# Unread matmuls in TensorE's waits, and another order of the last scatters, in a four-layer kernel with experts

## The chip, the cores and the metric

The kernel runs on one core of one Trainium2 chip. The metric is the device time of one execution in microseconds (us); the time before is the median of three runs. A profiled execution, of which the trace is kept, has a time of its own.

## What is computed

The input is x of 4 x 1024 tokens with 256 features. Four sub-layers follow each other, each as x = x + layernorm(f(layernorm(x))): a gated attention in groups of 64 with a cumulative linear part, a low-rank feed-forward, an attention of 16 heads with relu weights, and a layer of experts. The change touches the seam between the last two and the end of the last one:

```python
# attention: scores = relu(q k / 4), divided by their sum, times v
S = sigmoid(xt @ Wg).T                    # 8 experts x 4096 tokens
G, I = top_k(S, 1024)                     # each expert takes its 1024 best tokens
hid = gelu(ex @ W1[e] + b1[e])            # ex = xt[I], 1024 x 256 -> 1024
out = (hid @ W2[e] + b2[e]) * G[..., None]
new_x = zeros.at[I].add(out)              # summed over the experts
x = x + layernorm(new_x)
```

## The kernel before

The tokens are held in eight tiles xs[0..7] of 512 tokens (128 partitions x 4 x 256). TensorE, VectorE and ScalarE run in the order in which the program is written (manual schedule, L1040 and L1315); GpSimd's order is the program's too from the seventh expert on (L1753).

**The relu attention (to L1307).** A loop over batch, query half, head group and key tile does scores (L1226), relu, and one step later the weighting with v (L1242). Other work is kept in two lists of closures, `beside` (steps with matmuls) and `rest` (vector steps); `go_on` (L1255) takes one of `beside` and one or two of `rest` after each step of the loop. After the loop, `finish` (L1304) does the last weighting and puts `divide` in front of `rest`: transposes on VectorE (L1274, L1113) that make oT. Then `while beside or rest: go_on()` (L1305) works off the lists: the output projection of tile 7 (pt, L1128), the transposes and gate matmuls of tile 6 (tpg L1186, pg L1200), tile 7's two layernorms on VectorE, ScalarE and GpSimd, and tile 7's own tpg and pg.

**The gate (L1319 to L1438).** Sigmoid of the logits (L1346 to L1349); a transpose of the scores (scoreT, `by_token` L1354), which are stored beside the token rows in tok_d; 15 rounds of a search for the threshold of each expert, three compares with counts on VectorE and one small matmul with the 0/1 matrix same_b (pn, L1381) each; a mask, two matmuls for counts (pall L1409, pearly L1411), two scans, and a transpose of the places (placeT, L1354 again, called at L1432). From the places come hi and lo, and from these the list of an expert's tokens: 32 small matmuls (parts, L1478) fed by VectorE's compares (at, L1468), one matmul with fold (L1490), the index on VectorE, and eight indirect DMAs from GpSimd's queue that fetch the rows (got, L1502).

**The experts (L1676).** 16 units u, two for each expert, of 512 tokens: transposes of the fetched rows (`turn`, L1672), W1 (ph, L1690), gelu (L1697), W2 (py, L1713), and the scatter with addition into acc_d (L1732). The first unit is done in two halves. The list of the next expert is made inside the first unit of each expert.

**The last expert.** Its sums aren't scattered into acc_d. While it runs, all other rows of acc_d are read back tile by tile, normalised, added to x and stored (`all_stats`, `all_scaled`, `all_out`). For its own 1024 tokens, in eight groups k of 128, the accumulated rows are fetched (`fetch_acc`), the bias times the gate is added (`known`, L1589), then this expert's py (L1726), then statistics with a power on GpSimd (`chosen_stats`, L1543 to L1547: rsd), subtraction of the mean (L1598), the sum with x (`chosen_sum`, L1602), and a scatter from GpSimd's queue over rows of the output (`chosen_out`, L1606), which waits for all stores of `all_out`. The table `beside_last` (L1631) says after which step these are issued: (half, "f", i) after the i-th block of W1, (half, "i", i) after the sum of k = 4 x half + i. Engines take what they are issued in that order, so a power stands in GpSimd's queue behind the scatters that were listed before it.

## Time and profile before

| what | value |
|---|---|
| three runs | 1636.32, 1636.36, 1637.09 us (median 1636.36) |
| the profiled execution's own time | 1637.27 us |
| its span, first to last instruction | 1635.4 us |
| busy: PE, DVE, ACT, POOL | 1544.9, 920.3, 634.4, 403.1 us |
| mean granted TensorE clock | 0.974 |
| PE busy from 1090 to 1140 us | 8.9 us of 50 |
| end of PE's last matmul, of the last scatter's issue | 1622.58, 1629.75 us |

PE is TensorE's matmuls, DVE is VectorE, ACT ScalarE, POOL GpSimd, SP the engine that issues most DMAs. The clock is given as a share of full speed. A matmul of f32 operands is two records in the trace. "Idle before, releaser" says how long an engine had nothing to do before an instruction and what ended that.

### The profile page before, as it was taken

The numbers are of one execution on the slowest core, as the hardware profiler recorded it, in microseconds if no ns is written. First come the engines' busy times: TensorE is split into PE (matmuls) and PEld (weight loads), VectorE is DVE, ScalarE is ACT, GpSimd is POOL, SyncE is SP. The second block draws the span as 40 slices with busy tenths as digits, with TensorE's granted clock in tenths as the row PEclk, the third lists the DMA queues.
The fourth block names the chain that finished last, engine by engine and source line by source line (L and its number), as shares of the span: only waits on it lengthen the run. The fifth ranks groups of instructions, "written<-read, shape, count | busy, mean of one in ns | idle before, by whom it ended". The sixth has DMA issues, their size and how long they took to land.

```text
span 1635.4 us, 22372 instructions
## 1 busy us (share of the span) xinstructions
PE 1544.9 (94%) x8663; PEld 769.3 (47%) x8663; DVE 920.3 (56%) x2085; ACT 634.4 (39%) x1101; POOL 403.1 (25%) x439
## 2 busy tenths in 40 slices
PE   7999999999999999999999999941999999999996
PEld 4666666665222232222323222220757667566674
DVE  5555566663657787878787888868211212122145
ACT  3344444445444545454545454511121121211232
POOL 4123232322201020111111101110423324323554
PEclk9999999999999999999999999965899999999998
DMA  8300000000000000001010100040233233234364
GB/s 202 122 1 1 1 1 1 1 1 1 1 1 1 27 14 15 25 7 34 6 35 1 40 9 19 14 167 4 54 77 69 66 74 72 66 77 94 60 156 124
DMA packets 70069, 71.13 MB, mean 43 GB/s; under 512 B 23598, under 2 KB 62923, under 8 KB 69835
## 3 DMA queue, kind: packets, MB, share of 16 engines
q1 hardware_dynamic: 56080, 47.01, 9.3%
q0 software_dynamic: 13008, 21.77, 7.2%
q8 instruction: 68, 1.11, 0.3%
q10 hardware_dynamic: 874, 0.93, 0.2%
q14 instruction: 39, 0.31, 0.1%
HBM read 41.74 MB, written 27.95 MB: 43 GB/s over the span
## 4 chain that ended last, share of the span: by engine, by line
PE 90%; issue 4%; DVE 3%; POOL 1%; ACT 1%; DMA 1%; SPq 0%; POOLq 0%; ACTq 0%; DVEq 0%
PE sc L1226 16%; PE po L1242 16%; PE ph L1690 13%; PE py L1713 13%; PE py L792 4%; PE pg L684 3%; PE pv L700 3%; PE pt L1128 2%; PE ph L848 2%; PE po L764 2%; PE pv L373 2%; PE pq L349 2%; PE pq L869 2%; PE po L768 2%; PE pk L349 2%
## 5 line engine op out<-in xcount | busy, mean ns | idle before, releaser
L1236 DVE TENSOR_SCALAR w<-sc 128x1024 f32<-128x1024 f32 x256 | 312.6, 1222 | 97.5 <-PE sc L1226 65.1
L1235 ACT ACTIVATE w<-sc 128x512 f32<-128x512 f32 x512 | 277.9, 594 | 229.7 <-PE sc L1226 102.5
L1226 PE MATMUL sc<-qT,kT 32*128 32x512 f32 x2048 | 293.6, 639 | 1.5 <-ACT w L1235 0.8
L1242 PE MATMUL po<-w,vaug 128*17 128x512 f32 x2048 | 274.7, 598 | 1.3 <-DVE turned L1274 0.3
L1713 PE MATMUL py<-w,hid 128*128 128x256 f32 x1024 | 230.1, 380 | 0.0
L1690 PE MATMUL ph<-xT,w 128*128 128x512 f32 (+1 forms) x544 | 225.0, 572 | 0.5 <-DVE xT L1674 0.4
L1697 ACT ACTIVATE hid<-ph,mb 128x512 f32<-128x512 f32 (+1 forms) x136 | 90.0, 662 | 346.3 <-PE ph L1690 345.0
L1713 PEld LDWEIGHTS py<-w,hid 128*128 128x128 f32 x1024 | 191.1, 190 | 32.0 <-issue 7.3
L1226 PEld LDWEIGHTS sc<-qT,kT 32*128 32x128 f32 x2048 | 80.8, 183 | 184.9 <-issue 170.7
L1690 PEld LDWEIGHTS ph<-xT,w 128*128 128x128 f32 x544 | 104.8, 193 | 111.7 <-issue 107.6
L1242 PEld LDWEIGHTS po<-w,vaug 128*17 128x17 f32 x2048 | 35.3, 95 | 200.3 <-issue 171.0
L1732 POOL DMA_INDIRECT acc_d<-y,idx x56 | 88.5, 1580 | 156.6 <-issue 129.4
L1502 POOL DMA_INDIRECT got<-tok_d,idx x64 | 65.8, 1027 | 154.1 <-DVE idx L1492 137.0
L1730 DVE TENSOR_TENSOR y<-py,mb 128x256 f32<-128x256 f32 x56 | 23.4, 418 | 142.7 <-PE py L1713 140.6
L1674 DVE COPY xT<-tp 128x512 f32<-128x512 f32 (+1 forms) x34 | 22.3, 660 | 93.4 <-PE tp L1672 93.4
L1060 POOL TENSOR_TENSOR rsg<-veg,mhalf 128x1 f32<-128x1 f32 x32 | 17.7, 553 | 219.6 <-DVE veg L1059 219.6
L792 PE MATMUL py<-wo,oT 128*128 128x256 f32 x256 | 61.9, 385 | 0.0
L684 PE MATMUL pg<-nT,wh 128*128 128x512 f32 x128 | 60.5, 604 | 1.5 <-ACT nT L623 1.5
L700 PE MATMUL pv<-wh,nT 128*128 128x512 f32 x128 | 59.7, 592 | 0.0
L1492 DVE CAST idx<-parts 128x8 int32<-128x8 f32 x8 | 1.3, 167 | 101.8 <-PE parts L1490 101.8
L792 PEld LDWEIGHTS py<-wo,oT 128*128 128x128 f32 x256 | 47.3, 190 | 17.2 <-issue 9.4
L565 POOL TENSOR_TENSOR x<-x,y 128x1024 f32<-128x1024 f32 x14 | 32.9, 2352 | 73.3 <-ACT y L554 73.3
(275 smaller groups left out, 1888.8 us busy)
## 6 DMA issues: line engine op xcount, KB each, us to landing
w<-in_L_ffn_W_dram SPq DMA_DIRECT2D x16, 1024.0 KB, 5.7
x<-in_L_attn_x_dram SPq DMA_DIRECT2D x8, 512.0 KB, 4.8
acc_d<-logits SPq DMA_DIRECT2D x8, 512.0 KB, 4.2
x_d<-x SPq DMA_DIRECT2D x8, 512.0 KB, 2.9
tok_d<-hg SPq DMA_DIRECT2D x32, 128.0 KB, 1.7
back_w<-acc_d SPq DMA_DIRECT2D x6, 512.0 KB, 8.0
out_dram<-x SPq DMA_DIRECT2D x20, 128.0 KB, 1.7
out_dram<-back_w POOLq DMA_DIRECT2D x4, 512.0 KB
```

The lines of the kernel that those rows point to most:

```text
L684: nc.tensor.matmul(pg, lhsT=wh[:, c, HID + e * P : HID + (e + 1) * P], rhs=d["nT"][:, c, :], start=(c == 0), stop=(c == DC - 1),)
L700: nc.tensor.matmul(pv, lhsT=d["nT"][:, c, i * P : (i + 1) * P], rhs=wh[:, c, 0:HID], start=(c == 0), stop=(c == DC - 1),)
L792: nc.tensor.matmul(py, lhsT=d["oT"][:, e, :], rhs=wo[:, e, :], start=(e == 0), stop=(e == EC - 1))
L1226: nc.tensor.matmul(sc, lhsT=row["kT"][t][rows, r, kt * P : (kt + 1) * P], rhs=row["qT"][rows, t, qh * TB : (qh + 1) * TB], start=True, sto ...
L1235: nc.scalar.activation(w[:, j, :], sc, AF.Relu)
L1236: nc.vector.tensor_scalar(w[:, 2:4, :], pair, 0.0, None, ALU.max)
L1242: nc.tensor.matmul(po[32 * j : 32 * j + HD + 1, :], lhsT=row["v"][:, kt, HQ * t + 2 * j + r, :], rhs=w[:, j, :], start=(kt == 0), stop=(kt ...
L1502: return nc.gpsimd.indirect_dma_start(out=dst, out_offset=None, in_=rows[:, :], in_offset=self.at_chunk(c), bounds_check=NT - 1, oob_is_er ...
L1690: nc.tensor.matmul(ph, lhsT=w1[:, c, f * P : (f + 1) * P], rhs=xT[u][:, c, h * n : (h + 1) * n], start=(c == 0), stop=(c == DC - 1),)
L1697: nc.scalar.activation(hid[:, f, h * n : (h + 1) * n], ph, AF.Gelu, bias=mb1[:, e * FC + f : e * FC + f + 1])
L1713: nc.tensor.matmul(py, lhsT=hid[:, f, i * P : (i + 1) * P], rhs=w2[:, f, :], start=(f == 0), stop=(f == FC - 1),)
L1732: scatter = nc.gpsimd.indirect_dma_start(out=acc_d[:, :], out_offset=lists[e].at_chunk(k), in_=y, in_offset=None, bounds_check=NT - 1, oob ...
```

## The change

One helper is new: it issues n matmuls of 128 x 128 by 128 x 512, bf16, same_b with itself (as the moving operand repeated four times), into a PSUM bank that nobody reads. It is called at seven places, with 8, 63, 9, 13, 12, 15 and 4 matmuls (124 in all). The loop that works off `beside` and `rest` after the attention is split, so that two of the calls stand ahead of it and after the first emptying of `beside`. The table of the last expert lists `known` 4 to 7, `chosen_sum` and `chosen_out` at other steps and in another order within a step.

```diff
+    def keep_busy(bank, n):
+        for _ in range(n):
+            nc.tensor.matmul(
+                bank, lhsT=same_b, rhs=same_b.unsqueeze(1).to_broadcast([P, 4, P]), start=True, stop=True
+            )
...
         finish(*before)
+        idle = ps.tile([P, 2, TB], F32, tag="d", name="idle", bufs=2)[:, 0, :]
+        keep_busy(idle, 8)
+        while rest and not beside:
+            go_on()
+        while beside:
+            go_on()
+
+        keep_busy(idle, 63)
         while beside or rest:
             go_on()
...
             nc.vector.reciprocal(sc, sc)
+            idle = ps.tile([P, TB], F32, tag="idle", name="idle", bufs=1)
+            keep_busy(idle, 9)
...
             nc.tensor.matmul(pearly, lhsT=earlier_b, rhs=n, start=True, stop=True)
+            keep_busy(idle, 13)
...
                 place, by_token(upto, "placeT").rearrange("p k (s e) -> p (k s) e", e=NE), -1.0, None, ALU.add
             )
+            keep_busy(idle, 12)
...
-            (1, "f", 5): [(all_scaled, 7, front), (all_out, 6)],
+            (1, "f", 5): [(all_scaled, 7, front), (all_out, 6), (known, 4)],
             (1, "f", 6): [(all_scaled, 7, back), (chosen_less_mean, 0, 1, 2, 3)],
-            (1, "f", 7): [(all_out, 7), (known, 4, 5, 6, 7)],
-            (1, "i", 0): [(chosen_sum, 0, 1, 2, 3), (chosen_stats, 4), (chosen_less_mean, 4), (chosen_out, 0, 1, 2, 3)],
-            (1, "i", 1): [(chosen_sum, 4), (chosen_stats, 5), (chosen_less_mean, 5), (chosen_out, 4)],
-            (1, "i", 2): [
-                (chosen_sum, 5), (chosen_out, 5), (chosen_stats, 6), (chosen_less_mean, 6), (chosen_sum, 6), (chosen_out, 6)
+            (1, "f", 7): [(all_out, 7), (chosen_sum, 0, 1, 2, 3)],
+            (1, "i", 0): [(chosen_stats, 4), (chosen_less_mean, 4), (chosen_out, 0, 1), (known, 5), (chosen_sum, 4)],
+            (1, "i", 1): [
+                (chosen_stats, 5), (chosen_less_mean, 5), (chosen_out, 2, 3, 4), (known, 6, 7), (chosen_sum, 5),
             ],
+            (1, "i", 2): [(chosen_stats, 6), (chosen_less_mean, 6), (chosen_out, 5), (chosen_sum, 6), (chosen_out, 6)],
             (1, "i", 3): [(chosen_stats, 7), (chosen_less_mean, 7), (chosen_sum, 7), (chosen_out, 7)],
...
                 nc.tensor.transpose(tp[:, i, :], lists[e].got[q * NJ + i][:, c * P : (c + 1) * P], ident)
+                if u == 0 and c == 0 and i == 0:
+
+                    keep_busy(first, 4)
...
         lists[0].gather()
+        first = ps.tile([P, TB], F32, tag="mm", name="idle", bufs=3)
+        keep_busy(first, 15)
```

## The prediction

> **What bounds the kernel now.** I read the page's busy slices first, then the windows, the waits and the chain around the dip, then the time line of the end.

> ```profile
> PE   7999999999999999999999999941999999999996
> ...
> PEclk9999999999999999999999999965899999999998
> ```
> TensorE fills the span but for one dip (slices 26 to 28, about 1068 to 1155 us) and the last slice; in the dip its granted clock falls to half. Only these two places can be bought. Windows of 3.413 us, laid so that the clock changes at their edges (start:end, length, PE busy, ..., then clock, DMA share, GB/s):

> ```profile
> PE tpg L1186 <- DVE hg L1171: 14.8, 1, 14.8
> PE tp L1672 <- DMA got<-tok_d,idx: 4.6, 2, 3.7
> PE scoreT L1354 <- DVE sc L1349: 3.9, 1, 3.9
> PE placeT L1354 <- DVE upto L1428: 3.5, 1, 3.5
> PE parts L1478 <- DVE at L1468: 3.2, 1, 3.2
> PE pt L1128 <- DVE oT L1113: 2.3, 1, 2.3
> ```
> These six waits are where the fillers go; each is how long one may last. And the chain (start, us):

> ```profile
> 1149.16 9.44 PE ph L1690 x32
> ...
> 1159.43 7.14 PE ph L1690 x32
> ```
> The same 32 matmuls take 9.44 us from a cold start and 7.14 us warm. (Further pieces of the chain used below: pt's 14 records 4.99 us from 1071.49; the next expert's 32 parts matmuls, warm, 1.92 us.) At the end (time line; start, us, [idle before]):

> ```profile
> 1621.49 0.58 POOL L1547 TENSOR_TENSOR rsd<-ved,mhalf 128x1 f32<-128x1 f32 x1
> 1622.10 0.48 DVE L1602 SCALAR_TENSOR_TENSOR xg<-accg,rsd,xg 128x256 f32<-128x256 f32 x1 [2.46 <-POOL rsd L1547]
> ...
> 1625.83 0.48 DVE L1726 SCALAR_TENSOR_TENSOR accg<-py,got,accg 128x256 f32<-128x256 f32 x1
> ...
> 1628.70 1.05 POOL L1606 DMA_INDIRECT out_dram<-xg,idx  x1 [0.81 <-DVE xg L1602]
> ```
> PE's last matmul ends at 1622.58, but the last expert's k=7 sum (1625.83) stands on DVE behind waits for powers that stand on POOL behind scatters. ved of k=5 was written at 1617.17, its power ran at 1621.49.

> [...] the changes at 1071.88, 1075.29, 1082.12 and 1153.80 us are 1, 3 and 24 windows of 3.413 us apart from the first[...]. [...] The trace has none; it has 128-column bf16 ones at 1.92/32 = 60 ns warm, so 240 ns at most for four times the columns. I take 216 ns, 427 ns cold.

> **The change part by part,** against the profiled run's 1637.27 us (span 1635.4, 1.87 around it).

> (a) 8 fillers ahead of pt. 8 x 0.216 = 1.7 us in the 2.3 us until oT is ready (1071.49), so hidden; at half clock 3.4 us, 1 us too long, but the clock is high there. The window then holds 1.12 + 1.7 = 2.8 of 3.41 us, 83%, above the 76% that kept the clock. pt's 14 records then take 14 x 0.216 = 3.0 us plus about 0.2 to drain instead of 4.99: y's second half starts 1.75 us earlier. Everything behind it is a DVE chain up to hg, so the whole 1.75 us passes on. Bounds 0 (a run whose window fell otherwise has nothing to save) and 1.8.

> (b) 63 fillers behind pg. 63 x 0.216 = 13.6 us, in a wait of 14.8 us (1078.63 to 1093.43) that moves as a whole: hidden with 1.2 us to spare. At 240 ns it is 15.1 us, 0.3 us over; should the weight load of 128 columns not hide, about a quarter more (0.27 us each, an estimate from the 512-column price) and 17 us, 2.3 us over, and tpg, queued behind them, would be late by that. What comes out: tpg and pg at full clock. Tile 6 shows pg ending 1.10 us after its last hTg copy, tile 7 now 1.98; the 8 cold transposes (1.99 us) would end about 0.4 us sooner. Together 1.25 us; bounds 0.3 and 1.3, since the clock may fall again after the fillers, where by my count only about half of a window is busy.

> (c) 9 fillers ahead of scoreT: 1.9 us (3.8 cold) in 3.9 us. Nothing either way; scoreT isn't on the path, the bit search on DVE is.

> (d) 13 fillers behind pearly. The 15 rounds before leave PE busy under 12% of each window, so these start cold. At 427 ns, 13 are 5.5 us, and placeT waits only 3.54 us (1132.52 to 1136.06). If the clock rises u us after their start, they end at u + (13 - u/0.427) x 0.216 = 2.80 + 0.494u. With a rise needing a window 74% to 100% busy, u lies between 2.5 and 6.8, so placeT is 0.5 to 2.0 us late; mean about 1.4. Queued behind is only placeT, but place, part, hi, lo, the lists and the first gather all wait for it: the whole goes on the path. placeT itself, warm, saves 0.25. Net cost 1.15 us.

> (e) 12 fillers behind placeT: warm by then, 2.6 us in 3.25 us (1136.79 to 1140.04), hidden; cold 5.1 us, 1.9 over. parts at full clock ends perhaps 0.1 us earlier, since DVE's at feeds it in pieces.

> (f) 15 fillers behind the fold matmul and 4 behind the first transpose: 3.2 us between 1143.1 and 1146.76, then 0.9 us between 1147.2 and 1148.17, hidden when warm; their bank is a PE-written slot of ph's, no new wait on another engine. Cold 6.4 and 1.7 us, about 3.4 over together. What they buy: ph 9.44 to 7.14 = 2.30 us, and transposes plus copy 0.26 us. From there to 1622.58 PE is the bound, so 2.56 us reach the end. Bounds 1.5 and 3, by where the window falls.

> (g) The end's order. chosen_sum of 0 to 3 moves to (1,f,7): 4 x 0.41 = 1.66 us of DVE from 1610.0 to 1611.65, done before k=4's sum at 1612.26. known 5 to 7 move into DVE's free time of (i,0) and (i,1), 0.42 us each. So k=4's statistics follow its sum: power at 1613.6 instead of 1615.14 (its start in the time line). POOL's new queue, with scatters of 0.97 to 1.32 us, 0.30 between them, and powers of 0.59: power 4, 0.56 of gap, scatters 0, 1 to 1617.3; power 5 (ved at 1617.2) 1617.45 to 1618.0; scatters 2, 3, 4 to 1621.9; power 6 to 1622.45; scatters 5, 6 to 1625.2; power 7 to 1625.8, then as now 0.8 for xg and 1.05 for scatter 7: 1627.6 instead of 1629.75. No DMA is added and SP's stores keep their place; the last store was moving bytes until 1612.6, before scatter 0 at 1614.7. POOL is full from 1613.6 on, so it is the bound. Gain 2.1 us, bounds 0.5 and 2.6. The 5.65 us from the last scatter to the span's end stay.

> Sum: 1.75 + 1.25 - 1.15 + 0.1 + 2.56 + 2.1 = 6.6 us, 1637.27 - 6.6 = 1630.7. The median of the runs shown is 0.91 lower than the profiled run. If that is a constant of profiling, 1629.8; if the median run simply did not lose (a), 1636.36 - 4.86 = 1631.5. I keep 1630.7, between.

> **The rivals.**
> 1. Placement costs nothing: pn's rounds or an early edge keep (d) in its cover. Against: u must be under 1.5 us, and the windows of the rounds are nearly empty. 1630.7 - 1.4 = 1629.3.
> 2. Fillers dearer than 216 ns, so that the 63 outlast the wait by 2.3 us. Against: py's records run at 3.46/16 = 216 ns with a load each. 1633.0.
> 3. Half the gains were not there: (a) 0, the end 0.5 because POOL's gaps grow: 1637.27 - (1.25 - 1.15 + 0.1 + 2.56 + 0.5) = 1634.0.
> 4. Slower: the fillers of (d) to (f) don't raise the clock, for instance because their windows stay split by transposes and gaps (74% was too little once). [...] Then d costs 2.0, e 1.9, f 3.4 and buys nothing: -1.75 - 1.25 - 2.1 + 7.3 = +2.2, 1639.5. It decides once these overruns pass 5.1 us. Against: (d), placeT and (e) are over 6 us without a gap.

> **How the numbers follow.** Forecast 0.57; rivals 0.15, 0.12, 0.10, 0.06. The forecast's own spread is about 1629 to 1632.5. The range takes in rivals 1 to 3: 1627.8 (all upper bounds but the unknown offset) to 1634.3. About 0.2%, 3.3 us, can be told from no change: faster means under 1633.1, which the forecast, rival 1 and half of rival 2 give: 0.80; same 0.14; slower 0.06.

> **What would show it.** Right: clock 1.00 from 1068 to about 1100 us and from the list's matmuls on; pt's 14 records in about 3 us; ph's first 32 in 7.1; placeT waiting for PE, not DVE, 1 to 2 us after upto; last scatter starting about 4.0 us after PE's end instead of 6.1. Wrong: tpg waiting behind fillers, the transposes of the first expert behind the 15, or a low clock at the first ph.

## The result, and the profile after

The changed kernel takes 1632.21 us (median of 9 runs, 1631.01 to 1633.66), the kernel before 1636.92 us (9 runs beside them, 1636.14 to 1637.82): a ratio of 0.9971 [0.9962, 0.9979], 4.7 us less. The forecast was 1630.7 us, 6.6 us less. The profiled execution took 1633.18 us (before: 1637.27), its span is 1631.2 us, its mean granted clock 0.986 (before: 0.974). Below, a filler is one of the unread matmuls, "the 63" are those of the call with 63, warm means at full clock and cold at half.

The two lines of the page that stood first in the prediction, now of the changed kernel:

```profile
PE   7999999999999999999999999983999999999997
...
PEclk9999999999999999999999999995999999999999
```
The dip is narrower, and only one slice of low clock is left. It is the slice of the 15 rounds of the threshold search, where TensorE has next to nothing to do (0.24 of 3.41 us busy in the window from 1101.00 us, below).

What TensorE still waits for from 1060 to 1150 us (us, times, longest):

```profile
PE pall L1426 <- DVE tie L1424: 1.4, 1, 1.4
PE scoreT L1371 <- DVE sc L1364: 1.3, 1, 1.3
PE tpg L1193 <- DVE hg L1178: 1.1, 1, 1.1
PE parts L1497 <- DVE at L1487: 0.7, 1, 0.7
PE pt L1135 <- DVE oT L1120: 0.7, 1, 0.7
```
The wait of 14.8 us for hg is 1.1 us now. But placeT, which waited 3.5 us for upto, is gone from the list: it no longer waits for DVE. The time line shows why (start, us, [idle before]):

```profile
1069.41 1.90 PE L206 MATMUL idle<-same_b 128*128 128x512 bf16 x8
...
1077.79 13.77 PE L206 MATMUL idle<-same_b 128*128 128x512 bf16 x63
1092.65 1.43 PE L1193 MATMUL tpg<-ident,hg 128*128 128x128 f32 x8 [1.09 <-DVE hg L1178]
...
1130.30 5.33 PE L206 MATMUL idle<-same_b 128*128 128x512 bf16 x13
1133.42 0.42 DVE L1446 TENSOR_TENSOR upto<-upto,mask 128x256 f32<-128x256 f32 x1
1135.46 0.38 PE L1371 MATMUL placeT<-ident,upto 128*128 128x128 f32 x2
1135.68 2.75 PE L206 MATMUL idle<-same_b 128*128 128x512 bf16 x12
...
1141.99 5.04 PE L206 MATMUL idle<-same_b 128*128 128x512 bf16 x15
```
The 63 take 13.77/63 = 0.219 us each and end 1.09 us ahead of hg. Single fillers start 0.216 us apart at full clock (the 63) and 0.427 us apart at half (the 13 until the clock rises and the first 9 of the 15; the first gap of each is 0.38), which are the forecast's 216 and 427 ns. In the trace of before pt's 14 records (f32, 256 columns) have the same two distances. The 13 take 5.33 us: upto is ready at 1133.84, placeT starts at 1135.46, 1.62 us late. The 12 are warm. The 15 should have taken 3.2 us and took 5.04. The windows of 3.413 us show where the clock was (start:end, length, PE busy, ..., clock, DMA share, GB/s):

```profile
1070.28:1073.69 3.41, 2.75 (x13) 1.83 (x12) 1.95 (x4) 0.00 (x0) 0.00 (x0) 1.00 0.00 0
...
1097.59:1101.00 3.41, 1.32 (x7) 0.55 (x6) 3.29 (x9) 0.82 (x2) 0.00 (x0) 1.00 0.00 0
1101.00:1104.41 3.41, 0.24 (x2) 0.01 (x1) 2.99 (x16) 3.39 (x2) 0.00 (x0) 0.50 0.42 27
...
1131.72:1135.13 3.41, 3.41 (x10) 1.21 (x8) 2.02 (x4) 0.00 (x0) 0.00 (x0) 0.50 0.00 0
1135.13:1138.55 3.42, 3.30 (x17) 1.43 (x14) 2.48 (x8) 0.66 (x1) 0.00 (x0) 1.00 0.00 0
1138.55:1141.96 3.41, 2.46 (x33) 0.85 (x34) 2.29 (x4) 0.27 (x1) 0.00 (x0) 1.00 0.02 5
1141.96:1145.37 3.41, 3.41 (x10) 1.21 (x11) 0.17 (x1) 0.00 (x0) 2.33 (x2) 0.50 0.13 40
1145.37:1148.79 3.42, 3.12 (x17) 1.67 (x16) 0.64 (x2) 0.00 (x0) 2.54 (x3) 1.00 0.36 91
```
The clock holds through the projection (first row), falls behind the 9 fillers (39% busy), and rises at 1135.13, after a whole window of cold fillers (3.41 of 3.41 us busy). Then it falls once more at 1141.96: the window before that one holds the parts matmuls, which by their records keep PE 72% busy. The next full window raises it again at 1145.37, 3.3 us ahead of the first ph. The changes at 1101.00, 1135.13, 1141.96 and 1145.37 us are 10, 2 and 1 windows of 3.413 us apart. So ph is warm, as the chain of waits shows (start, us):

```profile
1148.63 7.17 PE ph L1712 x32
...
1156.63 7.14 PE ph L1712 x32
```
At the end (time line; PE's last matmul ends at 1605.81 + 13.98 = 1619.79):

```profile
1610.90 0.59 POOL L1566 TENSOR_TENSOR rsd<-ved,mhalf 128x1 f32<-128x1 f32 x1 [7.66 <-DVE ved L1565]
1612.74 1.16 POOL L1625 DMA_INDIRECT out_dram<-xg,idx  x1 [1.25 <-DMA out_dram<-x]
...
1620.84 0.48 DVE L1748 SCALAR_TENSOR_TENSOR accg<-py,got,accg 128x256 f32<-128x256 f32 x1
1624.53 1.05 POOL L1625 DMA_INDIRECT out_dram<-xg,idx  x1 [0.81 <-DVE xg L1621]
```
Power 4 stands ahead of the scatters, as planned, and the k=7 sum starts 1.05 us after PE's end instead of 3.25. The last scatter starts 4.74 us after PE's end instead of 6.12. But scatter 0 waited 1.25 us behind the power for the landing of a store of x, which before it did not (0.56 us there).

**A ruler for all runs.** Two executions are not aligned: the start of the kernel, which differs between executions even where it is not edited, moves the rest of the run by up to 1.75 us (last section). So every trace below is cut into stages between fixed events. B: from the start of the attention's last weighting (po) to pearly. C: from pearly to the first ph. D: from there to the start of the last 64 records of py. E: from their end to the last scatter. In us, each a difference of two starts in the time line:

| kernel | psim (start of run) | last po | B | C | D | E |
|---|---|---|---|---|---|---|
| before | 19.94 | 1067.52 | 64.95 | 16.69 | 459.44 | 6.12 |
| changed | 20.86 | 1068.43 | 61.84 | 18.36 | 457.18 | 4.74 |
| order_only | 19.77 | 1067.37 | 64.97 | 16.59 | 459.38 | 3.95 |
| short_fillers | 21.26 | 1068.83 | 63.25 | 16.71 | 459.25 | 5.35 |
| eight | 20.47 | 1068.06 | 61.86 | 16.46 | 457.20 | 3.83 |
| among_parts | 20.05 | 1067.62 | 61.87 | 18.22 | 457.15 | 3.85 |
| half_stores | 20.78 | 1068.34 | 61.85 | 18.31 | 457.22 | 3.89 |
| warm_start | 20.81 | 1068.37 | 61.84 | 18.42 | 457.19 | 3.84 |
| no_63 | 20.21 | 1067.75 | 63.21 | 16.79 | 457.15 | 3.85 |
| through_rounds | 20.02 | 1067.57 | 61.72 | 16.23 | 457.16 | 3.85 |
| warm_start_32 | 19.13 | 1068.39 | 61.88 | 18.47 | 457.19 | 3.84 |
| best | 19.25 | 1068.46 | 62.31 | 16.25 | 457.15 | 3.91 |
| transposes | 21.52 | 1069.09 | 61.87 | 18.03 | 457.22 | 3.85 |
| best_2 | 19.16 | 1067.24 | 62.22 | 16.21 | 457.17 | 3.89 |

From before to changed: B -3.11, C +1.67, D -2.26, E -1.38, together -5.08. The attention's end lies 0.91 us later in the trace of the changed kernel. That leaves 4.2 us, which is the difference of the spans.

### The profile page after: what moved, and what is told of

It is laid out like the page before. It is cut to its first block, busy times and chain, and to the rows that moved or that the text cites. A ratio compares the mean times of both kernels' runs of the same rounds, so it can differ in the third digit from the quotient of the medians.

```text
span 1631.2 us, 22623 instructions
## 1 busy us (share of the span) xinstructions
PE 1569.7 (96%) x8787; PEld 778.2 (48%) x8787; DVE 920.7 (56%) x2085; ACT 634.7 (39%) x1101; POOL 403.3 (25%) x439
## 3 DMA queue, kind: packets, MB, share of 16 engines
q8 instruction: 69, 1.13, 0.3%
## 4 chain that ended last, share of the span: by engine, by line
PE 92%; DVE 4%; issue 1%; POOL 1%; ACT 1%; DMA 1%; POOLq 0%; SPq 0%; DVEq 0%; ACTq 0%
PE sc L1233 16%; PE po L1249 16%; PE ph L1712 13%; PE py L1735 13%; PE pg L691 4%; PE py L799 4%; PE pv L707 3%; PE ph L855 2%; PE po L771 2%; PE pt L1135 2%; PE pv L380 2%; PE pq L356 2%; PE pq L876 2%; PE po L775 2%; PE pk L356 2%; PE pkv L786 1%
```

## The experiments

The theory: unread matmuls win where they keep or raise the clock (B and D), lose where they start cold and outlast the wait (C), and the end wins by itself, through GpSimd's queue. The rivals: the split loop or the new banks, not the clock, moved the first stages; the overrun in C has another cause; the rest of E is the store. All times are medians; each ratio is to the kernel before, on the same chip.

**order_only: only the new table.** The kernel before, with the last expert's table of the diff and without any filler.

> The kernel before with only the new table of the last expert, none of the fillers. If the gain splits as I read it (about 1.4 us at the end, about 3.7 us from the clock): the last scatter starts about 4.7 us after TensorE's last matmul instead of 6.1, everything ahead of it as before, and the time is about 1.4 us (0.1%) below the kernel before. Rival, that the order of the end is worth nothing by itself because the stores of the last tile bound it: last scatter still about 6 us after TensorE's end, time as before. Rival, that the end is the larger part: 3 us or more.

1635.06 us (21 runs, 1633.79 to 1636.10) beside 1637.33; 0.9986 [0.9979, 0.9992]. B, C and D are those of before, E is 3.95: the table alone gives 2.2 us of E and 2.3 us between the medians. That is within 0.1 us of the prediction's (g); the 1.4 us expected just above, read from the changed kernel's trace, was too little. Scatter 0 comes 0.67 us after power 4. The end's working was right; in the changed kernel 0.8 us of it was lost to the store.

**short_fillers: the same instructions with nothing in them.**

```diff
-                bank, lhsT=same_b, rhs=same_b.unsqueeze(1).to_broadcast([P, 4, P]), start=True, stop=True
+                bank[:, 0:4], lhsT=same_b, rhs=same_b[:, 0:4], start=True, stop=True
```

> The changed kernel with each filler cut from 512 columns to 4: the same 124 matmuls in the same places of the program, the same waits and buffers, next to no work for the array. If the gain at the seam comes from the granted clock: the clock falls to half as in the kernel before, the first expert's first 32 ph records take about 9.4 us instead of 7.2, tpg to logits about 4.6 us instead of 3.2, placeT waits for DVE again (not late by 1.6 us), and of 5 us of gain only about 1.4 us of the end are left. If the gain came from something else that the change brought (other buffers, split loops, order in the queue): most of the 5 us stays.

1635.69 us (13 runs) beside 1637.33; 0.999 [0.9982, 0.9998]. C is 16.71 and D 459.25, within 0.2 us of before: neither the banks nor the loops bought D, the filled time did, and the 13 cost nothing when they are short. One thing is against my working: B fell by 1.70 us. The 14 pt records were warm here too (3.29 us), behind an idle time of 2.09 us. So in this execution (a) came without the filled time of the 8, by where the window's edges fell (1071.07 and 1074.48, last section). Its first ph, and its scatter 0:

```profile
1148.79 9.23 PE L1712 MATMUL ph<-xT,w 128*128 128x256 f32 x32
...
1615.33 1.16 POOL L1625 DMA_INDIRECT out_dram<-xg,idx  x1 [1.61 <-DMA out_dram<-x]
```
The store was late here too, by more.

**eight: 8 fillers instead of 13 behind pearly.** At the measured 0.427 us 8 take 3.4 us, which fits the 3.54 us even cold.

```diff
-            keep_busy(idle, 13)
+            keep_busy(idle, 8)
```

> The changed kernel with 8 fillers behind pearly instead of 13. My reading: 13 cold ones made placeT about 1.4 us late, 8 of 427 ns are 3.4 us and fit into the 3.5 us until upto is ready. placeT then starts when upto is ready, the places come about 1.2 us earlier counted from pearly, the 12 behind it still end before parts, and the time is about 1.2 us below the changed kernel (a spread of about 2.5 us over its runs may hide that; the trace shows it). Rival: with 8 the clock isn't raised in time, the 12 run cold into parts, and what is won ahead of placeT is lost behind it.

1630.46 us (5 runs, 1630.07 to 1630.62) beside 1637.33; 0.9958 [0.9944, 0.9971]. C falls from 18.36 to 16.46. From the time line:

```profile
1129.95 3.57 PE L206 MATMUL idle<-same_b 128*128 128x512 bf16 x8
...
1133.56 0.69 PE L1371 MATMUL placeT<-ident,upto 128*128 128x128 f32 x2
1134.04 2.91 PE L206 MATMUL idle<-same_b 128*128 128x512 bf16 x12
1134.28 0.42 DVE L1449 TENSOR_SCALAR place<-placeT 128x256 int32<-128x256 f32 x1 [0.78 <-PE placeT L1371]
```
placeT starts when upto is there, place 1.25 us sooner after pearly than in the changed kernel (4.36 against 5.61), though placeT itself is cold (0.69 us, in the changed kernel 0.38). The rest of the 1.9 us is the 15, which here took 3.40 us: from the index to ph it takes 5.75 us instead of 6.40. The first part is owed to the edit. The second also comes in traces with 13 (see (f) below), so it isn't shown to be. In time the two intervals overlap.

**among_parts: fillers between the groups of parts matmuls,** against the fall of the clock at 1141.96.

```diff
-            keep_busy(idle, 12)
+            keep_busy(idle, 14)
...
             lists[0].collect(part)
+            keep_busy(first, 1 if part < 3 else 2)
```

(The tile `first` is set up ahead of this loop; that line is left out here.)

> The changed kernel with 14 instead of 12 fillers behind placeT, and one filler after each of the first three groups of the parts matmuls of the first list and two after the fourth. In the changed kernel the clock fell to half at the end of the window that held parts, 72% busy by the trace, so that the 15 fillers took 5.0 us instead of 3.2 and the first transposes came about 1 us late. If that window was too idle for the array: the clock stays at full speed from the 14 on to ph, the 15 take 3.2 us, ph starts about 5.7 us after the index instead of 6.4; about 0.2 us lost in parts, 0.4 us won in all. If the fall isn't decided by how full that window is, the clock falls again and ph starts no earlier.

1631.25 us (6 runs) beside 1637.33; 0.9966 [0.9954, 0.9978]. A miss. The clock stays up and the 15 take 3.40 us, so ph follows the index by 5.85 us instead of 6.40. But each filler holds up the next group (0.88 us apart instead of 0.62), and from place to the index it takes 7.18 us instead of 6.35. 0.55 us won, 0.83 lost. Even the 0.55 can't be put down to these fillers: six traces without them have the 15 at 3.40 us too.

**half_stores: the last tile's sum and store in two halves,** the first one a block of W1 earlier.

```diff
+        def half_out(tiles):
+            y = ys[NB - 1][0]
+            j = slice(tiles[0], tiles[-1] + 1)
+            x = xs[NB - 1][:, j, :]
+            nc.vector.tensor_tensor(x, x, y[:, j, :], ALU.add)
+            stores.append(nc.sync.dma_start(out_flat[NB - 1][:, j, :], x))
...
-            (1, "f", 6): [(all_scaled, 7, back), (chosen_less_mean, 0, 1, 2, 3)],
-            (1, "f", 7): [(all_out, 7), (chosen_sum, 0, 1, 2, 3)],
+            (1, "f", 6): [(all_scaled, 7, back), (chosen_less_mean, 0, 1, 2, 3), (half_out, front)],
+            (1, "f", 7): [(half_out, back), (chosen_sum, 0, 1, 2, 3)],
```

> The changed kernel with the last tile's sum and store in two halves, the first one step earlier. In the changed kernel's trace scatter 0 stood 1.25 us behind the first power, ended by a store's landing, where two other runs with the new order show 0.55. If the last store's landing is what is late next at the end: half the bytes remain after the second half's sum, scatter 0 stands 0.55 us behind the power, and the last scatter starts about 3.9 us after TensorE's end instead of 4.7; the time is 0.5 us or so below the changed kernel. If GpSimd's own queue is the bound whatever the stores do: no change against runs with a gap of 0.55, and gaps over 1 us still occur.

1632.21 us (6 runs) beside 1637.46; 0.9966 [0.9954, 0.9978]. Scatter 0 follows power 4 by 0.62 us and E is 3.89. That proves little: of the ten traces with whole stores and the new table (the changed kernel's among them), eight have 0.55 to 0.67 us as well, and only the changed kernel's and short_fillers' a late store. So how late the store lands differs between executions; the new order alone does not bring the wait. What the order changes is how early scatter 0 needs the store (see (g) below).

**warm_start: 24 fillers at the kernel's start,** from a tile set by a memset, since the window's place there moves the whole run (by up to 1.75 us, last section).

```diff
+    warm = const.tile([P, P], BF16, name="warm")
+    nc.vector.memset(warm, 1.0)
...
+    def warm_up(n):
+        for _ in range(n):
+            nc.tensor.matmul(
+                warm_bank, lhsT=warm, rhs=warm.unsqueeze(1).to_broadcast([P, 4, P]), start=True, stop=True
+            )
+    warm_up(10)
...
+    warm_up(14)
```

> The changed kernel with 24 more fillers at the kernel's start (a constant bf16 tile, 10 ahead of the first small transpose and 14 behind it), in TensorE's idle time until the first tile is normalised at 10.0 us. The first matmuls there run at half clock until 13.5 to 15 us, and the traces so far differ by up to 1.5 us in when this stretch ends. If that is the same price: psim starts at about 18 us instead of 19.8 to 21.3, the time is 2 to 3 us below the changed kernel, and the spread of its runs shrinks. Rival: the start is bound by the loads and by VectorE, not by TensorE's clock, and the time stays within 0.5 us; or the 14 are too many and delay the first transposes.

1631.75 us (5 runs) beside 1637.46; 0.9966 [0.9952, 0.9979]: no difference. The 24 ran from 1.05 to 8.5 us, PE was idle till 10.09, and the clock had fallen again by the first pg:

```profile
12.17 3.66 PE L708 MATMUL pg<-nT,wh 128*128 128x512 f32 x4 [0.43 <-ACT nT L647]
```

**no_63: without the 63 behind pg.**

```diff
-        keep_busy(idle, 63)
```

> The changed kernel without the 63 fillers behind the gate of tile 6. My reading: they bring about 1.4 us, by tpg and pg of tile 7 at full clock, and nothing more. Then from the last hg's transpose to the logits it takes 4.6 us instead of 3.2, the 9 fillers run cold and end at most 0.5 us after the sigmoid, and the time is 1.4 us above the changed kernel. Rival: the clock falls anyway between the fillers and tpg and they bring nothing; or they bring more, because the clock would otherwise stay low in the rounds too.

1631.55 us (5 runs) beside 1637.46; 0.9966 [0.9952, 0.998]. In the trace the expected loss is there: B is 63.21, 1.37 us more than with the 63; the 8 transposes take 1.99 us and pg 2.60, cold. In the time it is not, because C came out 1.57 us shorter in this run: the 13 took 4.37 us and the 15 3.40. By the line under (d) below, the 4.37 us stand for a clock that rose about 3 us after the start of the 13, not 4.83 (an estimate), and 5 runs don't tell 1.4 us from that.

**through_rounds: 6 fillers in each of the 15 rounds,** so that the clock is still up when pearly comes.

```diff
                 nc.tensor.matmul(pn, lhsT=same_b, rhs=n, start=True, stop=True)
+                keep_busy(idle, 6)
```

> The changed kernel with 6 more fillers behind the count matmul in each of the 15 rounds (1.3 us of the 1.8 us that TensorE waits for the next counts, at full clock). If the 13 fillers behind pearly are late only because they start at half clock: the clock stays at full speed through the rounds, the 13 take 2.8 us and end before upto, placeT waits for VectorE again, and the time is 1.2 to 1.6 us below the changed kernel. If the clock can't be held that way (a window with 65 to 80% of such work is too little, or the 6 start cold and stretch a round by 0.7 us): rounds of over 2 us and no gain.

1630.68 us (5 runs) beside 1637.46; 0.996 [0.9947, 0.9974]. The rounds take 1.98 us each as before, the mean clock is 0.998, C is 16.23:

```profile
1129.31 2.97 PE L206 MATMUL idle<-same_b 128*128 128x512 bf16 x13
...
1132.92 0.44 PE L1371 MATMUL placeT<-ident,upto 128*128 128x128 f32 x2 [0.64 <-DVE upto L1447]
```
The same 13 take 2.97 us instead of 5.33, and placeT waits for DVE again. With `eight` this settles the overrun: 13 are too many from a cold start and not too many from a warm one, and the bank has no part in it.

**warm_start_32: 32 fillers at the start,** the second call with 22.

> As the first try at the kernel's start, with 32 fillers instead of 24. There the 24 stood together from 1.05 to 8.5 us, TensorE was idle until 10.09, and the clock fell again at 12.17, so that pg's first four records took 3.66 us. 8 more at full clock end at about 10.2 us. If idle time ahead of the transposes was the cause: the clock holds, pg's first four take about 1.9 us, psim starts at 19.1 us or so instead of 19.8 to 21.3, and the time is 1 to 2 us below the changed kernel. If the transposes that follow (8, at 10.1 to 11.7 us) count too little as activity: the clock falls again at the end of the window that holds them and nothing is won.

1630.82 us (5 runs) beside 1636.98; 0.9961 [0.9947, 0.9974]. The first pg records are warm, and psim starts at 19.13, the earliest of all:

```profile
12.16 1.99 PE L708 MATMUL pg<-nT,wh 128*128 128x512 f32 x4 [0.43 <-ACT nT L647]
...
418.27 1.93 PE L1250 MATMUL sc<-qT,kT 32*128 32x512 f32 x6 [0.77 <-ACT w L1259]
420.13 1.91 PE L1266 MATMUL po<-w,vaug 128*17 128x512 f32 x8
```
Yet the attention ends where it ended without them (1068.39). The last two lines say where the lead went: at the seam from the first sub-layers to the relu attention the clock was at half for one window, 418.5 to 421.9 us (in the changed kernel these groups take 1.13 and 1.05 us). Against the changed kernel the lead was still 1.71 us at the start of the first of the two lines; at the next group it was 0.06.

**best: through_rounds, half_stores and warm_start_32 together.**

> The changed kernel with 6 fillers in each round of the search, the last tile's store in halves, and 32 fillers at the kernel's start. By my reading the rounds bring 1.5 us, the halves 0 to 0.8, the start 0 to 2: 1629.5 us, against 1632.2 for the changed kernel. The clock stays high from 1068 us to the end. If the parts don't add up, for instance because the saving in the rounds and the one at the end are the same luck of the window: 1631.

1630.48 us (5 runs) beside 1636.98; 0.9954 [0.9941, 0.9968]. Less than the sum: the clock fell at 418 us again (the same two groups take 2.06 and 1.76 us), and in the first rounds the fillers met a cold window (2.63 us for 6, later 1.46), which shows in B, 62.31.

**transposes: 126 transposes of f32 in place of the 63 fillers,** since the slower rival named transposes among what keeps the clock from rising.

```diff
-        keep_busy(idle, 63)
+        for _ in range(126):
+            nc.tensor.transpose(idle[:, 0:P], ident, ident)
```

> The changed kernel with 126 f32 transposes of 128 x 128 in place of the 63 fillers behind the gate of tile 6 (0.109 us each at full clock, 13.7 us in all). A look at what holds the clock, not at the time. If transposes count as activity like other matmuls: the clock stays at full speed through them, and tpg of tile 7 starts as in the changed kernel. If they don't: the clock falls at the end of the first window full of them, the rest run at about 0.22 us each, they end up to 12 us late, and tpg with them.

One run, 1632.74 us. B is 61.87, that of the changed kernel:

```profile
1078.44 13.97 PE L1320 MATMUL idle<-ident 128*128 128x128 f32 x126
1093.34 1.42 PE L1193 MATMUL tpg<-ident,hg 128*128 128x128 f32 x8 [0.92 <-DVE hg L1178]
```
Transposes of f32 held the full clock through 14 us, 0.111 us each.

**best_2: best, with 3 fillers ahead of the attention's first scores and 3 behind them.**

```diff
         before = None
+        keep_busy(po, 3)
...
                         if before is not None:
                             finish(*before)
+                        else:
+                            keep_busy(po, 3)
```

> As best, with six more fillers at the other seam: 3 ahead of the relu attention's first scores and 3 behind the first step's scores, in waits of 0.7 and 0.8 us. In the traces of best and warm_start_32 the 1.7 us that were ahead at psim (19.1 instead of 20.9) were still ahead at 388 us and gone at 443, and the clock was at half from 418.7 to 421.5 us in warm_start_32, which the other traces don't have there. If that fall, by the window's place, is where the start's saving went: the clock holds, the last weighting of the attention ends 1.6 us earlier than in best, and the time is 1628.9. If the saving is lost to something else ahead of the attention: the same 1630.5 as best.

1629.48 us (5 runs, 1629.29 to 1630.05) beside 1636.99; 0.9955 [0.9942, 0.9969]. The clock stays up at the seam (1.00 from 400 to 463 us), and the attention ends 1.2 us sooner than in `best` (1.6 expected). On its page no slice is left low:

```profile
PE   9999999999999999999999999998999999999997
...
PEclk9999999999999999999999999999999999999999
```
A slice is 41 us long, so this hides one window at half clock in the first rounds, 1100.60 to 1104.02 us. The median is the lowest measured, about 2.7 us under the changed one's, though from another group of runs, and the intervals of the ratios overlap in part. Its ratio is no better than that of `best` (0.9955 and 0.9954), so the times don't tell these two apart.

## Why the prediction was right and where it was wrong

The forecast was right in its kind and 1.5 us too good: 1632.21 against 1630.7, within the range. The gain between the medians, 4.7 us, fell 1.9 us short of the 6.6, since the median before lies 0.35 us under the profiled run that the forecast was counted from. Of the signs of being right, the clock up to about 1100 us, pt, ph and placeT came as named. Two did not come in this trace: the clock did not stay up from the list's matmuls on, and the last scatter started 4.74 us after PE's end, not 4.0. One sign of being wrong came too, the first transposes behind the 15. Step by step, with the stages of the table:

- **(a), 1.75 us forecast.** 1.68: pt's 14 records took 3.30 us instead of 4.99. `short_fillers` got the same without filled time, so that execution did not need the 8. One whose window falls as in the kernel before shows what they do. In `through_rounds` the window 1068.48 to 1071.89 starts 0.91 us after the start of the last weighting (before: 0.95). With the 8 it is 81% busy instead of 33%, and the clock holds in the next one, which before had half:

```profile
1068.48:1071.89 3.41, 2.75 (x16) 1.41 (x13) 2.66 (x5) 0.00 (x0) 0.00 (x0) 1.00 0.00 0
1071.89:1075.31 3.42, 3.42 (x19) 2.87 (x18) 1.78 (x4) 0.01 (x1) 0.00 (x0) 1.00 0.08 28
```

In all eleven traces with the 8 at full length pt's 14 records take 3.29 us.
- **(b), 1.25.** 1.42, from the start of tpg to the logits; `no_63` loses 1.37. The fillers cost 0.219 us each and ended 1.09 us early (1.2 forecast).
- **(c), nothing.** The 9 took 2.10 us in the wait for the scores and left 1.26 us of it.
- **(d), -1.15.** -1.25. The clock rose 4.83 us after the start; the line 2.80 + 0.494u gives 5.19 us for the 13, measured 5.33. In the seven traces with a cold start of the 13 they took 4.37 to 5.63 us, and `eight` and `through_rounds` took the loss away from two sides.
- **(e), 0.1.** Nothing: hidden, but the parts matmuls took 2.44 us as before; DVE feeds them (a group every 0.62 us).
- **(f), 2.56: the first step that failed in size.** ph warm gave 2.27 us (2.30 forecast). The 0.26 us of warm transposes became a loss of 0.43: from the index to ph 6.40 us, before 5.97. I had the clock up from (d) on. It fell again at the end of the window with the parts matmuls, the 15 ran at half speed for part of their time and held up the first transpose. In 4 of the 11 traces with these 15 they took 5.03 to 5.08 us, in 7 they took 3.40. The four are those in which one window held all 32 parts matmuls and next to no filler (0.05 us at most), and was 71 to 74% busy. In the seven the edge fell elsewhere, or fillers stood among the parts, and no window with parts was under 80% (`transposes`):

```profile
1139.82:1143.23 3.41, 2.73 (x35) 0.94 (x35) 2.03 (x5) 0.27 (x1) 0.00 (x0) 1.00 0.00 0
```

Which of the two an execution gets was not controlled. 0.69 us of the miss.
- **(g), 2.1: the second.** The queue on POOL went as worked out, powers and scatters in the order of the table (in the changed kernel's trace power 4 at 1610.90, scatters 0 and 1 at 1612.74 and 1614.19, power 5 at 1615.21): 3.83 to 3.95 us from PE's end to the last scatter in eleven traces, 4.0 forecast. In the changed kernel's trace it was 4.74, since a store of x landed late. I had read that it moved bytes until 1612.6, ahead of scatter 0 at 1614.7, and had said that it kept its place. That reading missed a thin rest, which in the trace of before moved until 1613.9 (22 GB/s in the first line, after 330 in the 1.5 us ahead of it):

```profile
1612.50:1614.00 1.50, 1.50 (x9) 1.32 (x8) 1.50 (x5) 0.00 (x0) 0.00 (x0) 1.00 0.07 22
1614.00:1615.50 1.50, 1.50 (x8) 1.33 (x7) 1.26 (x5) 0.00 (x0) 0.36 (x1) 1.00 0.00 0
```

In the changed kernel the last of it moved at 1611.5, in `short_fillers` at 1614.1, and scatter 0 started about 1.3 us later in both. By that figure (an estimate from these two traces) scatter 0 would have had to wait until about 1615.2 in the trace of before as well. The new order brought scatter 0 closer to the store, and I gave that no price. 0.72 us of the miss.

With 0.1 each from (d) and (e) and 0.1 the other way from (a) and (b), these make the 1.5 us between 6.6 and 5.08. That the level missed by the same 1.5 us is chance. The spans differ by 4.2, since the starts of the two traces lie 0.91 apart; the medians, over nine runs each, by 4.7. (The range's low end, 1627.8, comes out only with the 0.91 us of offset taken off as well; the upper bounds alone give 1628.7.)

Of the rivals, the first (nothing lost in C) is what `eight` and `through_rounds` made true by an edit: 1630.5 and 1630.7 us, where I had 1629.3. The second, dearer fillers, fell with 0.219 us. The third, half of the gains, is not what B, D and E show. The slower rival had its mechanism in part: a clock that doesn't stay up. It cost 0.4 us, not 7.3. One of its reasons, transposes, is not borne out: in `transposes` 126 of them in f32 ran at the full clock through 14 us, 0.111 us each.

What stays open: why a window full of parts matmuls, 71 to 74% busy, loses the clock when less busy ones keep it (last section; in the trace the form of its matmuls is 128 x 16, and whether that is the cause was not shown), and why the store of x has a slow rest in some executions. A version with the 13 cut to 8 and the rounds filled was not tried.

## What to carry to other kernels

Check whether unread matmuls fit their wait at the clock that they start with. Here 13 from a cold start took 5.33 us in a wait that had lasted 3.54 us and made placeT 1.62 us late. Either fewer of them (`eight`: 3.57 us) or a clock kept up through the idle stretch (`through_rounds`: 13 in 2.97 us) ended that. When a queue is reordered so that something comes earlier, price what it will now wait for next, even if that was done in time before, and follow a transfer to its last bytes. And cut the traces into stages between fixed events before two executions are compared: here the start alone moves the rest by more than most of the single steps.

## What the hardware showed that I had not expected

- **The start sets the run.** psim starts between 19.77 and 21.52 us in the traces of the ten kernels without start fillers, and the attention's last weighting follows it by 1047.54 to 1047.60 us in each. The first four pg records take 2.71 us in the trace of before and 3.58 in that of the changed kernel, by where the clock's window ends (the clock rises at 13.7 and 15.5 us by the traces' record of it). This alone is 1.75 us of spread, as much as a step here.
- **A lead can be lost again.** warm_start_32 won 1.7 us at the start and lost it 400 us later, at a seam where of the other traces only `best` loses the clock.
- **Busy share alone does not sort the windows.** Here windows with 33% and 39% lost the clock, those with 71 to 74% of narrow matmuls lost it too, and these two kept it. The first is 49% busy, with pt's matmuls (`short_fillers`). The second holds the end of the 63, transposes and the first gate matmul (changed kernel; same columns as above):

```profile
1071.07:1074.48 3.41, 1.68 (x8) 1.50 (x9) 1.69 (x4) 0.00 (x0) 0.00 (x0) 1.00 0.00 0
...
1090.76:1094.17 3.41, 2.29 (x13) 1.14 (x12) 2.52 (x10) 0.65 (x2) 1.66 (x3) 1.00 1.01 259
```
The second is 67% busy, and the clock is at full in what follows both: in `short_fillers` pt's 14 records take 3.29 us, and here pg's 8 records take 1.69 us at 1094.11, cold they took 2.60.
